# One decay in four moved from PSUM to SBUF for a fourth common PSUM bank, with the x projection ahead of the gates, a two-lane feed-forward and the second expert product by halves

## The chip, the cores and the metric

The kernel runs on one core of a Trainium2 chip, in fp32, as one launch. The metric is the device time in microseconds. Engines are named as the profile names them: PE (TensorE), PEld (its weight loads), DVE (VectorE), ACT (ScalarE), POOL (GpSimd) and SP (SyncE, which mainly issues DMAs).

## What is computed

Two "metaformer" layers on x of 4 batches, 384 channels, 32 x 32 positions. Each layer adds a token mixer and then a feed-forward part to x:

```python
x = x + _L0_conv_ref(_ln_c(x), ...)          # selective scan in four directions
t = _to_tokens(x)
t = t + _L0_ffn_ref(_ln_t(t), ...)           # 384 -> 1536 -> 384, weights are Kronecker products
x = _from_tokens(t, x)
x = x + _L1_conv_ref(_ln_c(x), ...)          # in_proj, causal conv, SiLU, selective scan, gate, out_proj
t = _to_tokens(x)
t = t + _L1_ffn_ref(_ln_t(t), ...)           # 4 experts, the best 2 for each token
```

The heart of both mixers is the selective scan over 1024 positions, with 16 states to a channel:

```python
dA = jnp.exp(dtt[..., None] * A)                         # decay
h = h * dA + (dtt * ut)[..., None] * bt[:, :, None, :]   # scan
y = jnp.einsum('bkdn,bkn->bkd', h, ct)                   # times C, summed over the 16 states
```

Layer 0 scans each batch in four directions (384 channels each). Layer 1 scans 768 channels once. The experts of layer 1 compute `gelu(x @ w1[e] + b1[e]) @ w2[e]` with w1 of 384 x 1536 and w2 of 1536 x 384.

## The kernel before, in words

**The scan as a stream of steps.** The scan is cut into 48 passes (a batch's half of 512 positions in one direction in layer 0, or a half of the channels in layer 1) and each pass into 12 steps: three groups of 128 channels by four groups of four states. That makes 576 steps. A step works on four tiles of 128 x 512, where a tile's partitions are 32 channels by 4 states. For each tile x of 0 to 3:

- ACT computes the decay, exp(dt * A), into `das[x]` (`decay`, L1497). The four `das` are PSUM banks.
- POOL has multiplied dt*u by B for the whole step before, in one instruction of 128 x 2048 into `s` in SBUF (`times_b`, L1491). Four such `s` go round in a ring.
- DVE runs the scan over the decay and `s` (`scan`, L1506). [...]
- DVE multiplies by C from PSUM into `s` (`times_c`, L1555), or POOL does it within `s` (`times_c_pool`, L1571). As a rule POOL takes the last tile alone (354 of 546 instructions), or the last two; in 30 steps DVE takes all four.
- PE sums the states of the four tiles into the bank `acc` (`add`, L1527). After four steps DVE gathers `acc` into the result.

Between passes' steps, ACT also keeps the last column as the state of the next half (`keep_state`, L1521).

**Everything else runs beside it.** Before a pass come the x projection (`prep_quad0`, `prep_quad1`: L579, L811) and the dt projection with softplus (`prep_pass`, L482 to L505); its results go to DRAM and are read back spread over partitions. In front of layer 1's scan of a batch stand the rest of layer 0 for that batch (`post0`: layer norm, GELU, adding x, layer norm, feed-forward in four rounds `ffn`, L649 to L706) and `prep1`: layer norm, then the in-projection and convolution of six chunks of 128 channels in two lanes `conv`, then the gates (z's half of the in-projection, SiLU, stored to DRAM) in two lanes `gate` (L766 to L789), and only then is the job `("pre", 1, b, h)` ended, for which layer 1's x projection waits. Behind the scan come `post1` (gate, out-projection, layer norm), `front` (routing of tokens to experts by indirect DMA), `experts` (blocks of 256 tokens, "pairs", or of 128, "lone" ones: 8 pairs and 3 lone blocks a batch) and `combine` (each token's two expert results, weighted).

**The order is made at build time.** A planner (`Plan`) runs an event simulation with hand-given costs (the numbers behind `yield PE, ...`), and emits each engine's instructions in the order it finds. The scan's steps are its main streams; the rest are lanes with ranks, experts lowest.[...]

**PSUM and other rooms.** There are eight banks: `acc`, four `das`, and three common ones in the free list `ps`, which all lanes use. An expert's bank is only taken if another stays free (`bank`, L1142), and the second product of a pair takes two at once (`bank(2)`, L1231), so all three must be free. When the scan is over, the `tail` job (L1463) gives the `das` to `ps`, and the scan's SBUF tiles to the lists of temporaries `tmp`, `t1` and of expert weights `mws`.

**Names of lines.** L1221 and L1241 are the experts' first and second products, L1187 their transposes, L1300 the copy of a block's result out of PSUM, L1332 and L1350 the indirect loads and products of `combine`. L671 and L682 are the feed-forward's products, L716 and L756 in-projection and convolution, L764 the convolution's SiLU, L780 and L783 the gates' copy and SiLU. L413 to L437 are layer norms, L1015 is a small cast in `front`. L1546 are products of zero weights that keep PE busy while it would wait (`fill`).

Of the kernel before, what the change touches and what calls it, by code (L numbers as in the profile page):

```python
# [36 lines left out]
NPAIR, NLONE = 8, 3  # L37
NBLK = NPAIR + NLONE
# [214 lines left out]
def layers(ctx, tc, ins, out, const):  # L253
# [47 lines left out]
    NK = T // P  # L301
    gates = {(b, h): wp.tile([P, NK, NE], F32, name=f"g{b}{h}") for b in range(NB) for h in range(NT)}
# [3 lines left out]
    tables = [wp.tile([1, 2, NBLK], I32, name=f"table{b}") for b in range(NB)]  # L306
    sels = tiles(2, [P, NK + 1, NE], "sel", pool=wp)
    b1s = tiles(3, [P, NF], "b1s", pool=wp)
    b2 = wp.tile([NE, D], F32, name="b2")
    nc.sync.dma_start(out=b2, in_=ins["b2"])  # L310
# [19 lines left out]
    pair_of = numbers(*range(NPAIR), 99, NPAIR, NPAIR)  # L330
    pair_at = numbers(*(2 * P * i for i in range(NPAIR)), 0, 2 * P * NPAIR, 2 * P * NPAIR + P)
    lone_of = numbers(*(NLONE + i for i in range(NPAIR)), *range(NLONE))
    floats = numbers(*[1] * NPAIR, *[0] * NLONE)
# [4 lines left out]
    ones = wp.tile([P, P], F32, name="ones")  # L338
    nc.vector.memset(ones, 1.0)
# [6 lines left out]
    nil = wp.tile([P, QP], F32, name="nil")  # L346
    nc.vector.memset(nil, 0.0)
    das = tiles(NG, [P, T], "da", pool=ps_1)
    ps = Free(tiles(3, [P, T], "ps", pool=ps_1))
# [42 lines left out]
    slot_y = [dram.tile([NE * SLOTS, D], F32, name=f"ys{b}") for b in range(NB)]  # L392
# [8 lines left out]
    def piece(dram_ap, c, h):  # L401
        return dram_ap[c * P : (c + 1) * P, cols(h)]
# [206 lines left out]
    def post0(b, h):  # L609
# [10 lines left out]
        def gelu():  # L620
            yield ACT, 3 * 0.82 + SWITCH
            for c in range(NC):
                nc.scalar.activation(y[:, c], y[:, c], AF.Gelu, bias=pv("lnb0", c, 1), scale=pv("lnw0", c, 1))
            exp_set()

        def add_x():
            for c in range(NC):
                xh = yield from t1.take()
                yield SP, land(256)
                nc.sync.dma_start(out=xh, in_=piece(x_in[b], c, h))  # L630
                yield POOL, 1.3
                nc.gpsimd.tensor_tensor(y[:, c], y[:, c], xh, ALU.add)
                t1.give(xh)

# [20 lines left out]
        def ffn():  # L655
            zg = st["zg", b]
            for i in range(NF // NC):
                w, proj1 = yield from wts.two()
                yield SP, land(192)
                nc.sync.dma_start(  # L660
                    out=w.rearrange("p a m -> p (a m)")[zrow, :], in_=ins["w_fc1"][:, i * NC * P : (i + 1) * NC * P]
                )
                nc.sync.dma_start(
                    out=proj1[:, :, :32],
                    in_=ins["w_proj1"][i * NC * P : (i + 1) * NC * P].rearrange("(f p) i -> p f i", p=P),
                )
                hid = yield from tmp.take()
                for j in range(NC):
                    ph = yield from ps.take()
                    yield PE, 1.1  # L670
                    nc.tensor.matmul(ph, lhsT=w[zrow, j, :], rhs=zg[zrow], start=True, stop=True)  # L671
                    yield ACT, 0.6
                    nc.scalar.copy(hid[:, j, :], ph)
                    ps.give(ph)
                wts.give(w)
                yield ACT, 1.5 + SWITCH
                nc.scalar.activation(hid, hid, AF.Gelu)
                exp_set()
                pr = yield from ps.take()
                yield PE, 3.0  # L680
                for j in range(NC):
                    nc.tensor.matmul(pr[grow], lhsT=proj1[:, j, :32], rhs=hid[:, j, :], start=j == 0, stop=j == NC - 1)  # L682
                tmp.give(hid)
                wts.give(proj1)
                if i == 0:
                    yield ACT, 0.6
                    nc.scalar.copy(zg[grow], pr[grow])
                else:
                    yield DVE, 0.65
                    nc.vector.tensor_tensor(zg[grow], zg[grow], pr[grow], ALU.add)  # L690
                ps.give(pr)
# [16 lines left out]
        return [ln1, gelu, add_x, ln2, ffn]  # L708
# [9 lines left out]
    def prep1(b, h):  # L718
# [6 lines left out]
        def conv(i):  # L725
            def gen():
                for j in range(NC):
                    c = i * NC + j
                    w, dg = yield from wts.two()
                    yield SP, land(192)  # L730
                    nc.sync.dma_start(out=w, in_=w_in[:, :, c * P : (c + 1) * P])
# [3 lines left out]
                    dg4 = yield from t1.take()  # L735
                    taps = [dg[:, 0, :], dg[:, 1, :], dg[:, 2, :], dg4[:, :P]]
# [21 lines left out]
                    wts.give(dg)  # L758
                    t1.give(dg4)
# [36 lines left out]
        return [ln, [conv(0), conv(1)], [gate(0), gate(1)], end]  # L796
# [114 lines left out]
    def front(u):  # L911
# [3 lines left out]
        def gen():  # L915
            b, h = u
# [82 lines left out]
            for j in range(NK):  # L999
                nc.tensor.matmul(  # L1000
                    pc[:, (j + 1) * NE : (NK + 1) * NE].rearrange("p (j e) -> p j e", e=NE),
                    lhsT=ones,
                    rhs=rep(sel[:, j], NK - j),
                    start=False,
                    stop=j == NK - 1,
                )
            yield DVE, 1.2
            so_far = nexts[b % 2] if h else base
# [3 lines left out]
            nc.vector.tensor_tensor(nexts[b % 2], pc[:, NK * NE : (NK + 1) * NE], so_far, ALU.add)  # L1012
# [3 lines left out]
            if h == NT - 1:  # L1016
                yield DVE, 6.0
                blocks(b, scratch, pg)
# [3 lines left out]
            yield from till(lambda: ("zero",) in plan.end and (b < 2 or ("read", b - 2) in plan.end))  # L1022
            t = 0.0
            for j in range(NK):
# [10 lines left out]
                for k in range(2):  # L1035
                    t = 3.0 + (yield POOL, 1.05, max(t, sent))
                    nc.gpsimd.indirect_dma_start(
                        out=slot_x[b % 2],
# [9 lines left out]
    def blocks(b, scratch, pg):  # L1048
# [26 lines left out]
        def within(at, first, end):  # L1075

            out, below = room("s", 1, NBLK, NE), room("p", 1, NBLK, NE)
            tt(out, lay(at, NE, True), lay(first[:1], NBLK, False), ALU.is_ge)
            tt(below, lay(at, NE, True), lay(end[:1], NBLK, False), ALU.is_lt)
# [4 lines left out]
        tt(cnt, nexts[b % 2], base, ALU.subtract)  # L1084
# [18 lines left out]
        tt(of_pair, of_pair, lay(off[:1], NBLK, False), ALU.mult)  # L1103
        at_pair = total("p", of_pair)
        at_s, number = room("s", 1, NBLK), room("p", 1, NBLK)
# [3 lines left out]
        last, number_s, no_pair = room("s", 1, 1), room("s", 1, NBLK), room("s", 1, NBLK)  # L1109
# [4 lines left out]
        tt(of_lone, of_lone, lay(off_lone[:1], NBLK, False), ALU.mult)  # L1114
# [4 lines left out]
        tt(of_lone, lay(at_lone, NE, True), lay(base[:1], NBLK, False), ALU.is_ge)  # L1119
        expert = total("p", of_lone)  # L1120
        nc.vector.tensor_scalar(expert, expert, -1.0, None, ALU.add)
        nc.vector.tensor_copy(tables[b][:, 0], at_lone)
        nc.vector.tensor_copy(tables[b][:, 1], expert)

    def experts():
        every = [(b, i) for b in range(NB) for i in range(NBLK)]
        size = [2] * NPAIR + [1] * NLONE
# [6 lines left out]
        def pressing():  # L1134

            done = [("gather", p0[NB - 1, 0]) in plan.end, ("pre", 1, NB - 1, 1) in plan.end]
            return done == [True, False]

        def known(b):
            return till(lambda: ("route", (b, NT - 1)) in plan.end)  # L1140
# [6 lines left out]
        def weights():  # L1147

            for b, i in every:
                yield from known(b)  # L1150
                yield SP, 1.0
                e = nc.sync.value_load(tables[b][:, 1, i : i + 1], min_val=0, max_val=NE - 1)
# [7 lines left out]
        def fetch():  # L1160

            for n, (b, i) in enumerate(every):
                yield from known(b)
# [3 lines left out]
                m = size[i]  # L1167
# [3 lines left out]
                yield SP, land(393), max(plan.end["route", (b, h)] for h in range(NT))  # L1171
                at = nc.sync.value_load(tables[b][:, 0, i : i + 1], min_val=0, max_val=NE * SLOTS - m * P)
                nc.sync.dma_start(
                    out=row, in_=slot_x[b % 2][bass.DynSlice(at, m * P)].rearrange("(s p) d -> p s d", p=P)
                )
                e = nc.sync.value_load(tables[b][:, 1, i : i + 1], min_val=0, max_val=NE - 1)
# [3 lines left out]
                if i == NBLK - 1:  # L1180
                    plan.end["read", b] = plan.now
# [18 lines left out]
        def work():  # L1200

            for n, (b, i) in enumerate(every):
# [4 lines left out]
                m = size[i]  # L1207
# [4 lines left out]
                for q in range(NQ):  # L1212
# [4 lines left out]
                    t = yield PE, 0.25 + 1.35 * m  # L1217
# [13 lines left out]
                py = (yield from bank(2)) if m == 2 else [(yield from bank())]  # L1231
                for q in range(NQ):
                    half_, at_ = divmod(2 * q, per)
                    yield from till(lambda: wq and half_ in made)
                    t, w = wq.pop(0)
                    yield "at", max(t, made[half_])
                    t = yield PE, 0.25 + 1.35 * m
                    w = w.rearrange("p (f d) -> p f d", f=2)
                    for f in range(2):
                        for k in range(m):  # L1240
                            nc.tensor.matmul(  # L1241
                                py[k][:, :D],
# [571 lines left out]
```

## Time and profile before

| What | Value |
|---|---|
| median of 3 runs (lowest to highest) | 5395.71 us (5385.36 to 5401.94) |
| the profiled execution | 5395.74 us, span 5394.0 us |
| mean granted TensorE clock | 0.918 |
| busy: PE, DVE, POOL, ACT | 4694.9, 4139.3, 3963.3, 3239.3 us |
| first and last scan instruction of the 48 passes | 82 (first `times_b`), 4567 us |
| `times_b` on POOL, L1491 | 576 x 4532 ns |
| scans on DVE, L1506, in PSUM | 801 x 1219 ns, 765 x 1286 ns (with a state) |
| scans on DVE, L1506, into SBUF | 351 x 1206 ns, 387 x 1275 ns (with a state) |
| products with C on DVE, L1555 | 1566 x 683 ns |
| decays on ACT, L1497 | 2304 x 686 ns |

How to read it: the first 4567 us are the stream of scan steps with everything else beside it; the last 827 us are the remaining experts and the combination of their results. Times in the text are in us from the span's start. A group's row has, after the bar, its busy time in us and the mean of one in ns. In the rows of stretches each engine's busy us stand with the number of its instructions, then the granted clock, the DMA share and GB/s. Records of neighbouring instructions of one engine overlap a little, so that their sum can exceed the time that they took.

### The profile page before, as it was taken

What the parts mean: (1) busy time and instruction counts of PE and PEld (TensorE: products, weight loads), DVE (VectorE), ACT (ScalarE), POOL (GpSimd) and SP (SyncE); (2) the same over time, 40 slices, a digit from 0 to 9 for tenths busy, and PEclk for the clock granted to TensorE, in tenths of its full rate; (3) what the DMA queues carried; (4) which work ended last, traced back from release to release, by engine and by line L of the source; (5) the groups of instructions that cost most, each with busy time, mean ns of one, the idle gap of its engine ahead of it and who ended that gap; (6) DMA issues with size and microseconds to landing.
All of it is one profiled execution on the core that took longest, in us unless ns stands there. A gap on an engine that the chain in (4) does not pass through costs nothing. (4 is left out here: it accounts for less than half of the span.)

```text
span 5394.0 us, 56734 instructions
## 1 busy us (share of the span) xinstructions
PE 4694.9 (87%) x17760; PEld 2159.8 (40%) x17760; DVE 4139.3 (77%) x4939; ACT 3239.3 (60%) x5776; POOL 3963.3 (73%) x1818
## 2 busy tenths in 40 slices
PE   9787787888888888989888888988899888999999
PEld 3222222222323333433444322333333345677776
DVE  5999999999999999488999999999993978100000
ACT  4454566765555777575666677776865645444342
POOL 4999998989898999388989889999983967200101
PEclk9889898899898989999999879999899999999998
DMA  3345555344444544546566444565534446556554
GB/s 123 126 153 187 186 190 188 123 157 145 151 137 150 185 150 138 164 154 200 180 197 215 148 130 147 170 201 172 166 126 148 153 171 204 174 179 216 168 172 160
DMA packets 425928, 890.56 MB, mean 165 GB/s; under 512 B 74485, under 2 KB 176025, under 8 KB 407193
## 3 DMA queue, kind: packets, MB, share of 16 engines
q1 hardware_dynamic: 368408, 695.53, 40.1%
q10 hardware_dynamic: 49024, 166.22, 8.9%
q0 software_dynamic: 8192, 25.17, 1.4%
q8 instruction: 141, 2.31, 0.2%
q14 instruction: 163, 1.33, 0.1%
HBM read 711.82 MB, written 174.95 MB: 164 GB/s over the span
## 5 line engine op out<-in xcount | busy, mean ns | idle before, releaser
L1491 POOL TENSOR_TENSOR s<-dtus,bt 128x2048 f32<-128x2048 f32 x576 | 2604.8, 4532 | 209.4 <-PE acc L1527 86.2
L1497 ACT ACTIVATE da<-dts,a 128x512 f32<-128x512 f32 x2304 | 1533.0, 686 | 1011.5 <-DVE s L1555 874.9
L1527 PE MATMUL acc<-s,four 128*32 128x512 f32 x4608 | 1062.9, 651 | 255.0 <-POOL s L1571 179.9
L1555 DVE TENSOR_TENSOR s<-da,ct 128x512 f32<-128x512 f32 x1566 | 1018.1, 683 | 51.3 <-ACT state L1521 50.6
L1546 PE MATMUL acc<-ident,nil 128*32 128x256 f32 x3980 | 978.5, 399 | 57.1 <-DVE big L601 22.3
L1571 POOL TENSOR_TENSOR s<-s,ct 128x512 f32<-128x512 f32 (+1 forms) x546 | 901.5, 1652 | 145.8 <-DVE s L1506 117.0
L1506 DVE TENSOR_TENSOR_SCAN da<-da,state,s 128x512 f32<-128x512 f32 x765 | 957.8, 1286 | 42.9 <-ACT ps L497 26.4
L1506 DVE TENSOR_TENSOR_SCAN da<-da,s 128x512 f32<-128x512 f32 x801 | 951.5, 1219 | 41.7 <-POOL s L1491 34.9
L1546 PEld LDWEIGHTS acc<-ident,nil 128*32 128x32 f32 x3980 | 436.7, 115 | 599.1 <-issue 183.0
L1527 PEld LDWEIGHTS acc<-s,four 128*32 128x32 f32 x4608 | 182.8, 111 | 834.2 <-POOL s L1571 395.8
L1506 DVE TENSOR_TENSOR_SCAN s<-da,state,s 128x512 f32<-128x512 f32 x387 | 484.3, 1275 | 0.1
L1506 DVE TENSOR_TENSOR_SCAN s<-da,s 128x512 f32<-128x512 f32 x351 | 417.3, 1206 | 4.9 <-ACT da L1497 4.8
L1221 PE MATMUL ps<-tmp,mw 128*128 128x256 f32 (+1 forms) x1728 | 376.6, 372 | 6.4 <-DVE tmp L413 2.2
L1241 PE MATMUL ps<-mw,tmp 128*128 128x384 f32 x1000 | 359.8, 505 | 8.6 <-DMA mw<-in_w_dram 4.9
L1221 PEld LDWEIGHTS ps<-tmp,mw 128*128 128x128 f32 x1728 | 305.9, 199 | 117.0 <-issue 28.7
L1355 DVE TENSOR_TENSOR tmp<-tmp,ps 128x384 f32<-128x384 f32 x16 | 8.8, 552 | 409.0 <-DMA dtus<-ys,slot 315.0
L1332 POOL DMA_INDIRECT tmp<-ys,slot x44 | 42.0, 956 | 370.0 <-ACT tmp L1342 319.9
L716 PE MATMUL ps<-big,w 128*128 128x512 f32 x576 | 285.8, 637 | 29.2 <-DMA w<-in_w_in_dram 17.6
L505 POOL TENSOR_TENSOR tmp<-tmp,big 128x256 f32<-128x256 f32 (+1 forms) x192 | 199.4, 1066 | 136.2 <-DVE tmp L499 136.1
L1241 PEld LDWEIGHTS ps<-mw,tmp 128*128 128x128 f32 x1000 | 187.9, 195 | 181.3 <-issue 54.0
L1355 DVE TENSOR_TENSOR s<-s,ps 128x384 f32<-128x384 f32 x2 | 1.1, 555 | 281.1 <-PE ps L1350 281.1
L482 PE MATMUL ps<-xd,dtw 12*128 12x512 f32 (+1 forms) x288 | 182.8, 718 | 30.1 <-DVE tmp L499 17.9
(364 smaller groups left out, 5703.0 us busy)
## 6 DMA issues: line engine op xcount, KB each, us to landing
mw<-in_w_dram SPq DMA_DIRECT2D x411, 384.0 KB
dtus<-dts SPq DMA_DIRECT2D x144, 1024.0 KB
dts<-dts ACTq DMA_DIRECT2D x288, 512.0 KB
dts<-tmp SPq DMA_DIRECT2D x384, 192.0 KB
bt<-rows SPq DMA_DIRECT2D x192, 256.0 KB
ct<-rows SPq DMA_DIRECT2D x192, 256.0 KB
dts<-in_w_dram SPq DMA_DIRECT2D x117, 384.0 KB
ys<-t SPq DMA_DIRECT2D x32, 768.0 KB
```

Of the source, the lines that this page charges most:

```text
L482: nc.tensor.matmul(pd, lhsT=dtw[dt_rows(q), c * P : (c + 1) * P], rhs=xd[dt_rows(q), cols(h)], start=True, stop=True,)
L505: nc.gpsimd.tensor_tensor(to, by, u[:, c], ALU.mult)
L716: nc.tensor.matmul(pi, lhsT=w[:, c, :], rhs=u[:, c], start=c == 0, stop=c == NC - 1)
L1221: nc.tensor.matmul(ph[:, k * width : (k + 1) * width], lhsT=w[:, c, k * P : (k + 1) * P], rhs=turned[:, c], start=c == 0, stop=c == NC - 1,)
L1241: nc.tensor.matmul(py[k][:, :D], lhsT=by_f(hids[half_], width)[:, at_ + f, k * P : (k + 1) * P], rhs=w[:, f], start=2 * q + f == 0, stop=2 ...
L1491: nc.gpsimd.tensor_tensor(ss[i % NSR], dtus[part_of(i) % 2], rep(bts[i % 4], NG), ALU.mult)
L1497: nc.scalar.activation(das[x], dts[(2 * part_of(i) + x // 2) % 3][:, x % 2, :], AF.Exp, scale=v["a"][:, g, m : m + 1])
L1506: nc.vector.tensor_tensor_scan(d if in_psum else s, d, s, 0.0 if v["first"] else state[:, v["slot"], j, x : x + 1], ALU.mult, ALU.add)
L1527: nc.tensor.matmul(acc[x * QP : (x + 1) * QP, :], lhsT=four, rhs=ss[i % NSR][:, x, :], start=m == 0, stop=m == 3)
L1546: nc.tensor.matmul(acc[:QP, : 2 * P], lhsT=nil, rhs=rep(ident, 2), start=fresh, stop=fresh)
L1555: nc.vector.tensor_tensor(ss[i % NSR][:, x, :], das[x], cts[i % 4], ALU.mult)
L1571: nc.gpsimd.tensor_tensor(s[:, m:, :], s[:, m:, :], rep(cts[i % 4], NG - m), ALU.mult)
```

## The change

1. `das[3]` becomes an SBUF tile, and `ps` has four banks. For the room in SBUF, some constants shrink to one column and are broadcast, `b2` is loaded at each combination, and the convolution's four tap matrices lie in one tile of `t1`, so a convolution takes one tile of `wts` in place of two.
2. `prep1` marks `("conv", b, h)` after the convolution's lanes; layer 1's x projection waits for this mark, and the gates come after it.
3. The feed-forward of `post0` runs as two lanes of two rounds each, in place of four rounds in a row; x is added by three lanes, which load it while the GELU is awaited.
4. The experts' second product is made in two halves of 192 columns. A half holds one bank, in which the two blocks of a pair lie side by side. The host lays w2 out accordingly.
5. Blocks are counted by groups of units (here a group is a batch, as before), the results' store has three buffers in place of four, and two planner costs and the copies' cost are set anew.

```diff
-    das = tiles(NG, [P, T], "da", pool=ps_1)
-    ps = Free(tiles(3, [P, T], "ps", pool=ps_1))
+    das = [*tiles(NG - 1, [P, T], "da", pool=ps_1), sp.tile([P, T], F32, name="da3")]
+    ps = Free(tiles(4, [P, T], "ps", pool=ps_1))
...
-    slot_y = [dram.tile([NE * SLOTS, D], F32, name=f"ys{b}") for b in range(NB)]
+    slot_y = [dram.tile([NE * SLOTS, D], F32, name=f"ys{g}") for g in range(3)]
...
-        def add_x():
-            for c in range(NC):
+        def add_x(c):
+            def gen():
                 xh = yield from t1.take()
                 yield SP, land(256)
                 nc.sync.dma_start(out=xh, in_=piece(x_in[b], c, h))
+                yield from till(lambda: ("gelu", b, h) in plan.end)
+                yield "at", plan.end["gelu", b, h]
                 yield POOL, 1.3
                 nc.gpsimd.tensor_tensor(y[:, c], y[:, c], xh, ALU.add)
                 t1.give(xh)
+
+            return gen
...
-        def ffn():
+        def ffn(lane):
+            def gen():
+                zg = st["zg", b]
+                for i in range(2 * lane, 2 * lane + 2):
...
-            for i in range(NF // NC):
...
-        return [ln1, gelu, add_x, ln2, ffn]
+        return [ln1, [gelu, *(add_x(c) for c in range(NC))], ln2, [ffn(0), ffn(1)], ffn_out]
...
-                    w, dg = yield from wts.two()
-                    yield SP, land(192)
-                    nc.sync.dma_start(out=w, in_=w_in[:, :, c * P : (c + 1) * P])
+                    w = yield from wload(w_in[:, :, c * P : (c + 1) * P])
...
-                    dg4 = yield from t1.take()
-                    taps = [dg[:, 0, :], dg[:, 1, :], dg[:, 2, :], dg4[:, :P]]
+                    dg = yield from t1.take()
+                    taps = [dg[:, tap * P : (tap + 1) * P] for tap in range(4)]
...
-        return [ln, [conv(0), conv(1)], [gate(0), gate(1)], end]
+        def mark():
+            plan.end["conv", b, h] = plan.now
+            return
+            yield
+
+        return [ln, [conv(0), conv(1)], mark, [gate(0), gate(1)], end]
...
-                py = (yield from bank(2)) if m == 2 else [(yield from bank())]
-                for q in range(NQ):
...
-                    t = yield PE, 0.25 + 1.35 * m
-                    w = w.rearrange("p (f d) -> p f d", f=2)
-                    for f in range(2):
-                        for k in range(m):
-                            nc.tensor.matmul(
-                                py[k][:, :D],
...
+                for part in range(2):
+                    py = yield from bank()
+                    for q in range(NQ // 2):
...
+                        t = yield PE, 0.1 + 1.32 * m
+                        w = w.rearrange("p (f d) -> p f d", f=4)
+                        for f in range(4):
+                            half_, at_ = divmod(4 * q + f, per)
+                            for k in range(m):
+                                nc.tensor.matmul(
+                                    py[:, k * HD : (k + 1) * HD],
...
+                    kq.append((t, g, i, part, py, at))
...
-                    yield ACT, 0.5
-                    nc.scalar.copy(row[:, :D], py[k][:, :D])
+                    yield ACT, 0.36 * m
+                    for k in range(m):
+                        nc.scalar.copy(rows[k][:, part * HD : (part + 1) * HD], py[:, k * HD : (k + 1) * HD])
...
+                b2 = flat[:NE, 2 * D + 3 * P :]
+                yield SP, land(6)
+                nc.sync.dma_start(out=b2, in_=ins["b2"])
...
-        q["need"] = ("pre", 0, b) if layer == 0 else ("pre", 1, b, x)
-        deps = [q["need"] if layer == 0 else ("pre", 1, b, x - 1) if x else ("post", 0, b, 0)] + ([("quad", n - 1)] if n else []) + ([("pass", p - 3)] if n > 1 else [])
+        q["need"] = ("pre", 0, b) if layer == 0 else ("conv", b, x)
+        deps = [q["need"] if layer == 0 else ("conv", b, x - 1) if x else ("post", 0, b, 0)] + ([("quad", n - 1)] if n else []) + ([("pass", p - 3)] if n > 1 else [])
...
-        ps.give(*das)
+        ps.give(*das[: NG - 1])
...
-        t1.give(*bts, *cts)
+        t1.give(*bts, *cts, das[NG - 1])
```

## The prediction, on record before the result

> **What bounds the kernel now.** I read the page's busy rows first, then the stretches between scan stops, then one plain step on VectorE and GpSimd.
>
> The page, busy tenths in 40 slices of 135 us: VectorE and GpSimd are full together until slice 34, then TensorE alone is.
>
> ```profile
> PE   9787787888888888989888888988899888999999
> DVE  5999999999999999488999999999993978100000
> POOL 4999998989898999388989889999983967200101
> ```
>
> The stretches (us, then busy us of PE, PEld, DVE, ACT, POOL): the two long stops of the scan, and what follows its last instruction at 4567.
>
> ```profile
> 2173.00:2256.00 83.00, 79.79 (x245) 38.51 (x243) 9.70 (x12) 42.36 (x70) 8.14 (x4) 0.98 0.59 188
> ...
> 4048.00:4159.00 111.00, 104.71 (x283) 44.09 (x281) 17.78 (x20) 51.56 (x77) 19.56 (x14) 0.98 0.53 167
> ...
> 4567.00:5394.00 827.00, 799.00 (x3418) 577.89 (x3416) 35.64 (x101) 331.97 (x566) 71.60 (x71) 0.95 0.58 181
> ```
>
> So the span is 82 us of start, 4485 us of scan (82 to 4567) and an 827 us tail that TensorE fills to 97%. In the scan lie five stops of 83, 33, 111, 33 and 12 us = 272 us; the other 4213 us carry 576 steps, 7.31 us each. In the same stretches without the four longer stops GpSimd is busy 1913.5 + 146.3 + 1455.7 + 155.6 + 166.7 = 3838 us, 6.66 us a step. Neither engine has much to give. A plain step, VectorE, then GpSimd:
>
> ```profile
> 3573.63 1.22 DVE L1506 TENSOR_TENSOR_SCAN da<-da,s 128x512 f32<-128x512 f32 x1
> 3574.76 1.20 DVE L1506 TENSOR_TENSOR_SCAN s<-da,s 128x512 f32<-128x512 f32 x1
> ...
> 3579.89 1.22 DVE L1506 TENSOR_TENSOR_SCAN da<-da,s 128x512 f32<-128x512 f32 x1
> ```
>
> ```profile
> 3572.88 4.53 POOL L1491 TENSOR_TENSOR s<-dtus,bt 128x2048 f32<-128x2048 f32 x1
> 3577.36 0.18 POOL L1570 COPY state<-s 128x1 f32<-128x1 f32 x1
> 3577.61 1.26 POOL L1571 TENSOR_TENSOR s<-s,ct 128x512 f32<-128x512 f32 x1
> ```
>
> The step is 6.26 us on VectorE (3573.63 to 3579.89) and 5.97 on GpSimd. The fourth scan (3574.76, `s<-da,s`) runs wholly inside GpSimd's `times_b` (3572.88 to 3577.41); GpSimd's `times_c` needs it next.
>
> **The fourth decay in SBUF.** This scan now reads both its streams, `da3` and `s`, from SBUF; until now every large VectorE operation had one operand in PSUM. The page has no such operation beside GpSimd. The nearest row is a small cast between two SBUF tiles, on VectorE and what GpSimd did then:
>
> ```profile
> 1645.19 3.30 DVE L1015 CAST slot<-t 128x8 int32<-128x8 f32 x1
> ```
>
> ```profile
> 1643.96 4.50 POOL L1491 TENSOR_TENSOR s<-dtus,bt 128x2048 f32<-128x2048 f32 x1
> ```
>
> Alone the cast takes 0.17 us. Here it ended at 1648.49, 0.03 after GpSimd's instruction (1648.46); at 2803 (1.83 us) and 4414 (2.04 us) it also ended 0.03 after the GpSimd instruction that was running. It was shut out for the whole instruction. That is one input in a copy, not two in a scan. [...] The scan rows of before, all with one input in PSUM, show no such wait (1.21 and 1.28 us). [...]
>
> Price: in the plain step GpSimd does 4.53 (`times_b`), then the fourth scan 1.15, hand-over about 0.25 (0.22 idle before the copy at 442.22, ended by the scan), then 0.18 + 1.26: 7.4 us in place of 6.26. Over all steps GpSimd's 6.66 + 1.15 + 0.25 = 8.06 us against 7.31: +0.75 x 576 = +430 us, the floor. On top come steps in which VectorE is the longer one all the same: around the waiting scan it has some 1.1 us of slack (7.4 - 6.26), and about 90 layernorm operations of 1.75 us exceed it by 0.65, +60; and GpSimd's own waits that are not this scan (136 us for L499's `tmp`, 86 for `acc`, 64 for `dtus`), of which I take some 110 to stay. Sum +600. The upper end: GpSimd's queue has 149 places where two `times_b` follow each other. If VectorE gets in only after both, it idles 3.4 us more at each of some 120: +400, so +1000. Behind the waiting scan stand on VectorE `mult` 2, the next step's scans and all gathers and layernorms; ACT's decays, `times_c`, TensorE's `add` and, through `acc` and the ring of four `s`, the next `times_b` wait for these. The 30 or so steps whose four products VectorE does itself (576 less 546 `times_c`) add a two-SBUF product of 0.68: within the rounding.
>
> Smaller: the decay's 0.69 us exponential writes SBUF, and the scan reads it there. [...] The trace has only the write side: 1206 ns to SBUF, 1219 to PSUM, -7 us. [...] ACT is 60% busy; a slightly longer exponential is hidden.
>
> **X projection ahead of the gates.** In the 83 us stop the last convolution's SiLU ends at 2160.9, the gates' six products and SiLUs run until 2190.5, the x projection (L811) starts at 2194.9. In the 111 us stop the same points are 4054.1, 4091.1, 4092.1. The gates' instructions (36 matmuls, 6 copies, SiLU, six weight loads on SP, a store on ACT's queue) all stay; they go beside the dt projection and the first scans, where TensorE waits for `add` and fills with idle products (L1546); on SP their weight loads now stand behind the pass's spreads, which costs nothing while post1 needs the gates only four passes (350 us) later. Without that cover the 33 to 37 us come back as a later end of the same chain. -33 and -37 us, and about as much in the two 33 us stops.
>
> **Two-lane feed-forward, add_x by three lanes, convolution with one weight tile in place of two.** Same instructions. In front of the 111 us stop one half's feed-forward runs from 3751 to 3893, 142 us for four rounds in a row; two lanes halve at most the waiting, -50 to -70, -40 where both halves compete for the four weight tiles. Together with the gates this exceeds each stop; the 50 us from x projection to first `times_b` (4098 to 4154) is next late and partly left. Of 272 us I take off 225 (bounds 120 and 265). The order is fixed at build time, so slower scans don't shorten the stops by themselves.
>
> **The fourth bank, second product by halves.** A pair of experts' blocks needed all three common banks free for its second product; now one of four suffices. Before, 33 of 76 result copies (L1300) were made by 4367, of 38 of the first two batches; those five are 2.5 pair blocks of 31 us (72 x 0.216 + 48 x 0.322 us, the chain's x24 5.18 and x16 5.16). That is 78 us that may leave the tail; I take -55. Against it: twice as many instructions of 192 columns for 384. By the chain's 0.216 us for 256 columns and 0.112 for 128 (x48 5.36) one takes 0.164: 96 x 0.164 = 15.7 for 15.5 us, +5 us in the tail. Weight loads double, but the 128-column case hides them already. So -50 (-130 to +60).
>
> At nothing: b2's 32 loads of 6 KB (issued before the indirect loads that take 3 us, so hidden; some 0.5 us of SP each if not), one store buffer fewer to zero, batch 3's results waiting for batch 0's combine (done by 3010), half-width copies (ACT is 40% busy in the tail).
>
> **Sum.** 5395.7 (span 5394.0 and 1.7 around it; the median is 5395.7 too) + 600 - 225 - 50 = 5720 us. About 0.3% (16 us) is what a measurement can tell from no change.
>
> **Rivals.**
> 1. VectorE slips in at each end of a GpSimd instruction, +600: 5720 (5600 to 5850). 0.47.
> 2. GpSimd's queued pairs go first: +880 to +1000: 5396 + 900 - 275 = 6020. For it: GpSimd's next instruction starts up to 0.04 us before the former's end. Against: the cast got in within 0.03. 0.19.
> 3. The floor, +430, and the whole 330 of gains: 5500. 0.15.
> 4. Not slower: the scan with two SBUF inputs does not wait for `times_b` (for it: no large row of before shows a two-input wait). Then 5396 - 225 - 50 - 20 = 5100. It decides from the point where the wait falls below 275 / 576 = 0.48 us a step. 0.17.
> The remaining 0.02 is a wait just at that point, no change.
>
> Faster 0.17, same 0.02, slower 0.81. The range leaves out case 4 and reaches from below case 3 into case 2: 5450 to 6080; the likeliest alone 5600 to 5850.
>
> **What would show it.** L1506 `s<-da` for the fourth decay with a mean of 2 us or more, where 1.21 and 1.28 stand now, each end 0.03 us behind an L1491; 7.4 us or more between L1491s in plain steps; the scan's end near 4940 and a tail near 780; stops of the scan under 50 us in sum; x projection within a few us of the convolution's SiLU. I am wrong if the fourth scan stays at 1.2 us (case 4), or if the steps pass 9 us (case 2). If the stops stay, the chain ahead of the convolution was late and not the gates.

## The result, and the profile after

The changed kernel takes 5878.35 us (median of 4 runs, 5874.78 to 5886.63) against 5390.53 us before (4 runs): the ratio is 1.0905 with a 95% interval of 1.088 to 1.093. It is slower by 9%. The profiled execution has a span of 5876.3 us.

The page of the changed kernel, busy tenths in 40 slices (of 147 us now). GpSimd, full before, is mostly at 7 to 8 in the scan; VectorE is at 9 nearly throughout, and of its dips at the long stops one is left.

```profile
PE   8777677787877788897878888888878877899999
...
DVE  5999999999999999996998999999999999610000
...
POOL 4878887888887887886787888888878788500101
```

Cut at the same places (first and last scan instruction; a stop is more than 3 us without a scan between two passes), the two spans differ like this. All values are read from the scans' times in the two traces:

| | first scan | stops | steps, us each | tail | span |
|---|---|---|---|---|---|
| before | 89 | 272 | 4207, 7.30 | 827 | 5394.0 |
| after | 90 | 57 | 4939, 8.57 | 790 | 5876.3 |
| difference | +1 | -215 | +732 | -36 | +482 |

TensorE's granted clock is lower too, 0.884 in the mean where it was 0.918. The steps don't wait for it: VectorE, which gathers TensorE's sums, is idle for 157 us of all the steps, 168 before.

VectorE's groups of the changed kernel (count, busy us, mean ns, idle before). The scans that write SBUF (their product with C is GpSimd's), 1206 and 1275 ns in the kernel before, are the ones to look at.

```profile
L1601 DVE TENSOR_TENSOR s<-da,ct 128x512 f32<-128x512 f32 x1560 | 1078.2, 719 | 30.6 <-ACT state L1567 30.1
L1552 DVE TENSOR_TENSOR_SCAN da<-da,s 128x512 f32<-128x512 f32 x799 | 972.7, 1245 | 11.7 <-ACT da L1543 7.9
L1552 DVE TENSOR_TENSOR_SCAN da<-da,state,s 128x512 f32<-128x512 f32 x761 | 956.9, 1286 | 25.1 <-POOL s L1537 14.6
L1552 DVE TENSOR_TENSOR_SCAN s<-da,state,s 128x512 f32<-128x512 f32 x391 | 791.0, 2043 | 5.3 <-ACT da L1543 5.3
L1552 DVE TENSOR_TENSOR_SCAN s<-da,s 128x512 f32<-128x512 f32 x353 | 722.2, 2062 | 0.4 <-ACT da L1543 0.4
```

These two rows hold third tiles as well, whose decay is still in PSUM. Of the fourth tile alone (every fourth scan in order) the mean is 2.36 us, 1.24 before, and 384 of the 576 exceed 1.45 us. A waiting instruction counts as busy here: the waits stand in its duration, not in the idle column (5.3 and 0.4 us for the last two rows). That is why VectorE looks full.

One such scan, on VectorE and then what GpSimd did:

```profile
4416.93 1.22 DVE L1552 TENSOR_TENSOR_SCAN da<-da,s 128x512 f32<-128x512 f32 x1
4418.06 3.11 DVE L1552 TENSOR_TENSOR_SCAN s<-da,s 128x512 f32<-128x512 f32 x1
```

```profile
4415.57 4.51 POOL L1537 TENSOR_TENSOR s<-dtus,bt 128x2048 f32<-128x2048 f32 x1
4421.23 0.18 POOL L1616 COPY state<-s 128x1 f32<-128x1 f32 x1 [1.15 <-DVE s L1552]
```

`times_b` ends at 4420.08, the scan at 4421.17, 1.09 us later: it did its work only then. GpSimd meanwhile stood idle for 1.15 us, as its next instruction needs this scan. It also goes the other way. Here the scan has waited for the end of `times_c` at 4060.40 and goes first, and the `times_b` that comes second takes 5.43 us in place of 4.53:

```profile
4060.01 1.46 DVE L1552 TENSOR_TENSOR_SCAN s<-da,s 128x512 f32<-128x512 f32 x1
```

```profile
4058.05 2.35 POOL L1617 TENSOR_TENSOR s<-s,ct 128x1024 f32<-128x1024 f32 x1
4060.35 5.43 POOL L1537 TENSOR_TENSOR s<-dtus,bt 128x2048 f32<-128x2048 f32 x1
```

All 384 long scans end 1.08 us after the end of a GpSimd instruction, within 0.014 us; only 7 let another boundary between two GpSimd instructions pass first. 323 of them began inside `times_b`. What the fourth scans take beyond 1.25 us sums to 640 us of waiting.

### The profile page after: what moved, and what is told of

It is laid out like the page before. It is cut to its first block, busy times and chain, and to the rows that moved or that the text cites. A ratio compares the mean times of both kernels' runs of the same rounds, so it can differ in the third digit from the quotient of the medians.

```text
span 5876.3 us, 60149 instructions
## 1 busy us (share of the span) xinstructions
PE 4864.8 (83%) x19390; PEld 2455.7 (42%) x19390; DVE 4864.0 (83%) x4933; ACT 3252.2 (55%) x5850; POOL 4120.6 (70%) x1811
## 5 line engine op out<-in xcount | busy, mean ns | idle before, releaser
L1537 POOL TENSOR_TENSOR s<-dtus,bt 128x2048 f32<-128x2048 f32 x576 | 2682.1, 4665 | 178.3 <-PE acc L1573 127.6
L1573 PE MATMUL acc<-s,four 128*32 128x512 f32 x4608 | 1161.5, 674 | 445.6 <-POOL s L1617 206.3
L1601 DVE TENSOR_TENSOR s<-da,ct 128x512 f32<-128x512 f32 x1560 | 1078.2, 719 | 30.6 <-ACT state L1567 30.1
L1552 DVE TENSOR_TENSOR_SCAN s<-da,state,s 128x512 f32<-128x512 f32 x391 | 791.0, 2043 | 5.3 <-ACT da L1543 5.3
L1552 DVE TENSOR_TENSOR_SCAN s<-da,s 128x512 f32<-128x512 f32 x353 | 722.2, 2062 | 0.4 <-ACT da L1543 0.4
L1253 PE MATMUL ps<-tmp,mw 128*128 128x256 f32 (+1 forms) x1872 | 402.8, 372 | 22.0 <-DVE tmp L511 9.0
L1275 PE MATMUL ps<-mw,tmp 128*128 128x192 f32 x2144 | 392.8, 340 | 11.5 <-ACT tmp L1321 10.1
L1275 PEld LDWEIGHTS ps<-mw,tmp 128*128 128x128 f32 x2144 | 364.9, 198 | 73.7 <-issue 39.3
L1401 DVE TENSOR_TENSOR tmp<-tmp,ps 128x384 f32<-128x384 f32 x19 | 10.4, 547 | 352.5 <-PE ps L1396 348.3
L1616 POOL COPY state<-s 128x1 f32<-128x1 f32 (+1 forms) x269 | 51.6, 192 | 321.5 <-DVE s L1552 316.8
L780 PE MATMUL ps<-tmp,t 128*128 128x512 f32 x384 | 200.4, 671 | 44.2 <-ACT tmp L773 40.8
```

What stands on the lines that cost most here:

```text
L780: nc.tensor.matmul(pk, lhsT=taps[tap], rhs=xt[:, tap : tap + T], start=tap == 0, stop=tap == 3)
L1253: nc.tensor.matmul(ph[:, k * width : (k + 1) * width], lhsT=w[:, c, k * P : (k + 1) * P], rhs=turned[:, c], start=c == 0, stop=c == NC - 1,)
L1275: nc.tensor.matmul(py[:, k * HD : (k + 1) * HD], lhsT=by_f(hids[half_], width)[:, at_, k * P : (k + 1) * P], rhs=w[:, f], start=4 * q + f ...
L1537: nc.gpsimd.tensor_tensor(ss[i % NSR], dtus[part_of(i) % 2], rep(bts[i % 4], NG), ALU.mult)
L1552: nc.vector.tensor_tensor_scan(d if in_psum else s, d, s, 0.0 if v["first"] else state[:, v["slot"], j, x : x + 1], ALU.mult, ALU.add)
L1573: nc.tensor.matmul(acc[x * QP : (x + 1) * QP, :], lhsT=four, rhs=ss[i % NSR][:, x, :], start=m == 0, stop=m == 3)
```

## The experiments

Each run's time is a median; the span of its profiled execution is cut as above. The base for all ratios is the kernel before on the same chip.

| Run | Time, us | stops | us a step | tail |
|---|---|---|---|---|
| decays in PSUM, three banks | 5299.22 | 85 | 7.41 | 847 |
| fourth decay in SBUF alone | 6074.48 | 288 | 8.49 | 809 |
| after, three banks | 5958.17 | 82 | 8.56 | 849 |
| after, `times_b` in two | 5730.89 | 47 | 8.34 | 787 |
| after, `times_b` only writes | 5211.48 | 31 | 7.47 | 786 |
| x projection ahead alone | 5352.60 | 214 | 7.35 | 832 |
| lanes alone | 5325.67 | 158 | 7.38 | 821 |
| both, product whole | 5355.84 | 101 | 7.38 | 908 |
| lanes and halves | 5312.17 | 130 | 7.41 | 830 |
| three decays in turn, four banks | 5332.07 | 63 | 7.62 | 795 |
| the same, ACT's side work patient | 5485.48 | 257 | 7.54 | 794 |

### All decays back in PSUM, three common banks

```diff
-    das = [*tiles(NG - 1, [P, T], "da", pool=ps_1), sp.tile([P, T], F32, name="da3")]
-    ps = Free(tiles(4, [P, T], "ps", pool=ps_1))
+    das = tiles(NG, [P, T], "da", pool=ps_1)
+    ps = Free(tiles(3, [P, T], "ps", pool=ps_1))
```

> The changed kernel with all four decays back in PSUM and three common banks; the rest of the change stays. Theory A (the two-SBUF scan is shut out while GpSimd's instruction runs): the 696 us of waits of VectorE go, steps are back near 7.3 us, the stops stay short, 5100 to 5220 us. Rival B (the steps are longer because the fourth bank lets more side work and experts between them): without the fourth bank the stops come back to 150 us or more and the steps shorten too, 5250 to 5400 us. Rival C (the chain edits themselves are worth nothing): 5380 to 5400.

5299.22 us, ratio 0.984 (0.983 to 0.986). Steps fall from 8.57 to 7.41 us, (8.57 - 7.41) x 576 = 670 us, and the stops stay short at 85 us. VectorE's groups of this run:

```profile
L1552 DVE TENSOR_TENSOR_SCAN s<-da,state,s 128x512 f32<-128x512 f32 x390 | 486.3, 1271 | 3.6 <-ACT da L1543 3.5
L1552 DVE TENSOR_TENSOR_SCAN s<-da,s 128x512 f32<-128x512 f32 x364 | 432.7, 1207 | 5.0 <-ACT da L1543 4.9
```

So the loss goes with the SBUF decay, and the rest of the change gains 1.6% even without the fourth bank. The time is 80 us above theory A's range: stops 85 and a tail of 847, both longer than with the fourth bank. The expectation had counted neither.

### The fourth decay in SBUF alone

The same move in the kernel before, with three common banks and one bank unused. The small constants and `b2` are as in the change: without them the scan's tiles would need 202.03 KB of SBUF a partition, and 200.22 are left.

```diff
-    das = tiles(NG, [P, T], "da", pool=ps_1)
+    das = [*tiles(NG - 1, [P, T], "da", pool=ps_1), sp.tile([P, T], F32, name="da3")]
```

> The kernel before with only the fourth decay in SBUF (and, for its room there, the small constants as single columns and b2 loaded at each combination); three common banks, the freed one unused, the instruction order that of before. Theory A (the two-SBUF scan is shut out while GpSimd's instruction runs): steps of 8.45 to 8.6 us, stops near 270 and tail near 827 as before, 6040 to 6130 us, and the fourth scan at a mean of 2.2 us or more. Rival B (the longer steps come of the fourth bank and the side work it lets in): under +150, 5400 to 5540 us.

6074.48 us, ratio 1.127 (1.125 to 1.130), as theory A has it. Rival B, that side work through the fourth bank lengthens the steps, is out: the side work is that of before here, and the steps are 8.49 us, 683 us more in all. The fourth scan's mean is 2.39 us. The two rows that hold it, third tiles included:

```profile
L1507 DVE TENSOR_TENSOR_SCAN s<-da,state,s 128x512 f32<-128x512 f32 x387 | 780.1, 2037 | 0.1
L1507 DVE TENSOR_TENSOR_SCAN s<-da,s 128x512 f32<-128x512 f32 x344 | 731.3, 2141 | 0.8 <-ACT da L1498 0.8
```

### The changed kernel with three common banks

```diff
-    ps = Free(tiles(4, [P, T], "ps", pool=ps_1))
+    ps = Free(tiles(3, [P, T], "ps", pool=ps_1))
```

> The changed kernel with three common banks in place of four, the fourth decay still in SBUF, one bank unused. If the bank is worth what the run with all decays in PSUM lacked (stops 85 for 57 us, tail 847 for 790), the time is 5878 + 85 = 5940 to 5990 us with steps near 8.6 us. Rival B (the bank's side work lengthens the steps): steps fall under 8.3 us and the time to 5800 or less. If the bank does nothing: 5870 to 5890.

5958.17 us (ratio 1.106). Steps are unchanged (8.56), stops +25, tail +58: the bank is worth 80 us. That is what it was bought for; its price was 670.

### times_b in two instructions

```diff
-        nc.gpsimd.tensor_tensor(ss[i % NSR], dtus[part_of(i) % 2], rep(bts[i % 4], NG), ALU.mult)
+        for g in range(0, NG, 2):
+            of = slice(g, g + 2)
+            nc.gpsimd.tensor_tensor(ss[i % NSR][:, of], dtus[part_of(i) % 2][:, of], rep(bts[i % 4], 2), ALU.mult)
```

> The changed kernel with times_b as two instructions of 128x1024 in place of one of 128x2048. Theory A: the longest wait behind it halves from 4.5 to 2.3 us and VectorE gets in between the two; the waits fall from 640 us to 350 to 450, against some 50 us more on GpSimd for the second instruction: 5650 to 5800 us. [...]

5730.89 us, ratio 1.064 (1.062 to 1.066), 147 us under the changed kernel. The waits fall from 640 to 491 us, less far than expected. Behind `times_b` a wait is 1.22 us in the mean where it was 1.83, but there are as many of them (343, 323 before). Part of the gain goes back on GpSimd: its waits for the scan fall from 674 to 354 us, but 262 of its 1152 halves take over 2.5 us where 2.36 is the rule, 231 us in all (77 us with whole `times_b`). The length of the instruction matters, and each of the 431 long scans still ends 1.08 us behind the end of a GpSimd instruction.

### times_b that only writes

```diff
-        nc.gpsimd.tensor_tensor(ss[i % NSR], dtus[part_of(i) % 2], rep(bts[i % 4], NG), ALU.mult)
+        for _ in range(2):
+            nc.gpsimd.memset(ss[i % NSR], 0.5)
```

> The changed kernel with times_b replaced by two memsets of the same tile on GpSimd: the product of dt*u and B is left out, so that GpSimd only writes SBUF in that place; times_c still reads. If a GpSimd instruction that reads is what shuts the two-SBUF scan out: no wait of the fourth scan behind the memsets, those behind times_c and the dt*u products stay (0.3 us or less a step in the mean, fourth scan under 1.6 us). If any GpSimd instruction does: waits behind the memsets too, each as long as what is left of the memset, fourth scan near 2 us.

5211.48 us in one run; the product of dt*u and B is left out. The fourth scan's mean is 1.28 us and its waits sum to 28 us (640 in the changed kernel). GpSimd is less full, 3474 us busy for 4121, but its memsets still run beside the scans: 219 fourth scans began with more than 0.3 us of a memset still to run, and took 1.23 us in the mean and 1.29 at most. All 35 that exceed 1.45 us waited behind a GpSimd instruction that reads SBUF. ACT still writes the fourth decay to SBUF here, so that write is not the cause. The memsets, and then the fourth scans with the third tiles on VectorE:

```profile
L1538 POOL MEMSET s<- 128x2048 f32 x1152 | 2073.4, 1805 | 266.0 <-PE acc L1574 220.5 <-DVE da L1553 10.5 <-PE acc L1593 1.3
```

```profile
L1553 DVE TENSOR_TENSOR_SCAN s<-da,state,s 128x512 f32<-128x512 f32 x391 | 499.3, 1298 | 7.7 <-ACT da L1544 7.7
L1553 DVE TENSOR_TENSOR_SCAN s<-da,s 128x512 f32<-128x512 f32 x353 | 429.4, 1234 | 2.6 <-ACT da L1544 2.0 <-ACT state L1568 0.4
```

So in this run the scan was held up by GpSimd instructions that read SBUF (all 35 waits that bring a scan over 1.45 us), not by the memsets, which only write it (1.29 us at most). The small cast, on which the prediction leaned, behaves otherwise: one of these waited behind a memset, on VectorE and then on GpSimd:

```profile
2789.31 0.56 DVE L1043 CAST slot<-t 128x8 int32<-128x8 f32 x1
```

```profile
2786.17 3.67 POOL L1538 MEMSET s<- 128x2048 f32 x2
```

It ends 0.03 us behind the memset, at 2789.87. So the cast's wait is not that of the scan, and the cast was no proof of it.

The run also gives the size of the fourth rival: the change without its waits is 5211 us here, not 5100. The run with all decays in PSUM says the same: 5299 less the 80 us of the bank is 5219.

### X projection ahead alone, lanes alone, and both

The kernel before with only the mark behind the convolution:

```diff
-        return [ln, [conv(0), conv(1)], [gate(0), gate(1)], end]
+        return [ln, [conv(0), conv(1)], mark, [gate(0), gate(1)], end]
```

> The kernel before with only the x projection ahead of the gates. By the prediction's working: 30 to 37 us off each of the four longer stops, 260 us of stops to some 130: 5250 to 5290 us. Rival (the convolution's end is late for the feed-forward ahead of it, and the gates' products move into the next chain): under 50 us gained, 5345 or more.

5352.60 us, ratio 0.993 (0.992 to 0.995): 33 us, a quarter of what was expected, as the expectation's rival has it. The x projection does move: in the first long stop it ends at 2147.6, 2.8 us behind the convolution's SiLU. But `times_b` starts at 2230 only. TensorE after it, in this run (L816 is the x projection, L716 the gates' products, L482 the first dt projection):

```profile
2144.86 2.78 PE L816 MATMUL ps<-big,w 128*56 128x512 f32 x6 [0.33 <-ACT big L764]
...
2149.45 5.42 PE L716 MATMUL ps<-big,w 128*128 128x512 f32 x12
...
2161.25 7.08 PE L716 MATMUL ps<-big,w 128*128 128x512 f32 x12 [2.60 <-DMA w<-in_w_in_dram]
...
2172.05 1.12 PE L482 MATMUL ps<-xd,dtw 24*128 24x512 f32 x2
```

Two thirds of the gates go ahead of the dt projection. From the x projection's end to `times_b` it now takes 82 us, where it took 51 before (2200.3 to 2251.7), as the lines of the kernel before and then `times_b` of both show. Of these 31 us, 14 lie ahead of the first dt projection (24.4 us for 10.4); the other 17 lie behind it and were not taken apart.

```profile
2194.89 5.36 PE L811 MATMUL ps<-big,w 128*56 128x512 f32 x12
...
2210.69 1.12 PE L482 MATMUL ps<-xd,dtw 24*128 24x512 f32 x2
```

```profile
2251.66 8.98 POOL L1491 TENSOR_TENSOR s<-dtus,bt 128x2048 f32<-128x2048 f32 x2 [18.79 <-DMA dtus<-dts]
```

```profile
2229.94 8.98 POOL L1496 TENSOR_TENSOR s<-dtus,bt 128x2048 f32<-128x2048 f32 x2 [21.00 <-DMA dtus<-dts]
```

The stop of 83 us became 78, that of 111 became 82, those of 33 became 17 and 37.

The lanes (feed-forward, adding x, one weight tile in the convolution) without the mark and without halves:

> The kernel before with only the two-lane feed-forward, the three lanes that add x and the convolution with one weight tile; decays in PSUM, three common banks, second product whole, gates ahead of the x projection. With the run of the x projection alone (stops 272 to 214 us) and the run of both (stops 101, tail 908) it makes a square. If the two add up: stops near 160 us, and the time 5355 to 5385 us as the tail grows by most of what the stops lose. If each stop is set by the later of two chains, so that only both together shorten it: stops over 200 us, 5375 or more.

5325.67 us, ratio 0.989 (0.986 to 0.992). The two stops of 83 and 111 us are down to 10 and 8; what is left, 46 and 81 us, stands before the second halves' passes. The time is 30 us below the expected range, as the tail did not grow (821). Stops add up (-58 and -114, together -171), times don't: both together, with the product whole, gave 5355.84 us (ratio 0.994), because the tail grew to 908 us.

> The run with all decays in PSUM and three common banks, with the second expert product as before (whole, two banks for a pair). If halves help with three banks (one bank of two free, in place of three of three): fewer copies done before the scan's end, a tail over 880 us, 5330 to 5400 us. If they only cost their instructions in the tail: 5280 to 5295 us. Stops and steps within 20 us of the run with halves either way.

The halves bring that tail to 847 and the time down by 57 us: beside the scan 31 of 76 results were made without them, 36 with them (72 half copies). This fits the bank that a half doesn't hold, though without the mark they make one result more only (38 for 37). Their instructions cost nothing that shows: 16 of 192 columns take 2.60 us, 0.1625 each.

Lanes and halves without the mark:

> The run with all decays in PSUM and three common banks (5299 us), with the gates again ahead of the x projection: lanes and halves alone. The x projection ahead took 33 us by itself, but on top of the lanes it shortened the stops by 57 us and lengthened the tail by 87. If halves mend that tail (907.9 to 847.0 us with x ahead), x ahead is worth its 57 us of stops less some tail: this version 5310 to 5350 us. If the experts' time beside the scan is what counts: 5270 to 5295 us, with a tail under 810.

5312.17 us, ratio 0.984 (0.982 to 0.986): within noise of the version with the mark, and half a per cent below the lanes alone. On top of lanes and halves the x projection ahead takes 45 us off the stops and gives 17 back in the tail, and no gain can be told.

### Three decay banks in turn, with four common banks

A way to keep the bank and all decays in PSUM: the n-th tile of the whole stream takes bank n mod 3, and a decay waits for the tile three before it.

```diff
+    def bank_of(i, x):
+        return das[(NG * i + x) % 3]
...
-            free = [("da free", i - 1, x)] if i else []
+            k, y = divmod(NG * i + x - 3, NG)
+            free = [("da free", k, y)] if k >= 0 else []
```

> The changed kernel with three decay banks in PSUM used in turn (tile n of all tiles takes bank n mod 3), no decay in SBUF, and the four common banks kept. Theory A: no wait behind GpSimd; with the bank's 85 us it would give 5299 - 85 = 5215 us if decays come in time. The rival for this version: a decay can start only when the tile three before it is through, so that ACT has some 0.6 to 1 us in hand where it had 2.4 or more, and each longer instruction of ACT (GELU, table loads, some 130) holds VectorE up by 2 us: 5400 to 5500 us, with L1506's successor idle on ACT's decays.

5332.07 us, ratio 0.989 (0.987 to 0.991), between the two cases expected. The bank pays (stops 63, tail 795), but steps are 7.62 us, +0.21 x 576 = 119 us against the run with four decay banks. VectorE's waits in this run say why:

```profile
DVE da L1555 <- ACT da L1546: 123.5, 52, 8.5
DVE s L1555 <- ACT da L1546: 97.4, 43, 9.5
```

Letting ACT's side work wait 14 us in place of 6 brings these to 78.3 and 72.8 us, but the chains ahead of layer 1 get late and the stops are back at 257 us: 5485.48 us, ratio 1.017, 85 us above the worse case expected.

> The run with three decay banks in turn and four common banks (5332 us), with the planner letting side work on ACT wait 14 us in place of 6 before it goes ahead of the decays. If ACT's side work is what holds the decays up (123.5 + 97.4 us of VectorE's idle time): those fall under 120 us and the steps to 7.5 us, 5260 to 5310 us, unless the chains ahead of layer 1 get late (stops over 120 us), then 5330 to 5400.

The fastest versions found are the change with its decays left in PSUM and three common banks, with or without the x projection ahead: ratio 0.984.

## Why the prediction was right, and where its terms were off

The direction, the mechanism and the range held: 5878 in 5450 to 6080, though above the likeliest case's own 5600 to 5850.

- **The fourth scan waits for `times_b`: right, but priced on the wrong engine.** That it would wait was the author's estimate from the cast; the longest fourth scan before took 1.35 us. +600 was forecast for the steps, +732 came. The move made 670 of these (8.57 against 7.41 us a step with all decays in PSUM); the other 62 came with the new side work, which the forecast put at nothing. The forecast followed GpSimd's step, 8.06 us for 7.31, and gave VectorE 1.1 us of slack around the waiting scan. VectorE has no such slack. In the two longest stretches of steps, before and then after, it is busy 96 to 97% (the length, then PE, PEld, DVE):

```profile
82.00:2173.00 2091.00, 1725.26 (x6477) 644.41 (x6476) 2006.45 (x2293) 1292.46 (x2330) 1913.49 (x846) 0.90 0.47 157
2449.00:4048.00 1599.00, 1380.15 (x5051) 576.79 (x5050) 1529.79 (x1753) 1107.69 (x1971) 1455.68 (x640) 0.90 0.52 170
```

```profile
90.00:2696.00 2606.00, 2052.66 (x7420) 800.44 (x7417) 2538.99 (x2469) 1452.70 (x2637) 2151.36 (x924) 0.87 0.43 138
2740.00:5086.00 2346.00, 1920.92 (x7354) 921.88 (x7354) 2254.38 (x2232) 1422.95 (x2565) 1881.40 (x806) 0.88 0.48 156
```

Over all steps VectorE's busy time grows by 742 us, 640 of them the scan's waits, and its idle time falls by 11 only: the steps got longer by the whole of the waits. A third of the scans did not wait (when 176 of these 192 began, no GpSimd instruction had more than 0.3 us left to run), and two thirds waited 1.67 us in the mean. GpSimd is not full: its waits for this scan grew from 169 (117 and 52) to 674 us, as its two rows in the list of waits show. That the sum came near is in part luck.

```profile
POOL s L1617 <- DVE s L1552: 357.1, 201, 10.3
...
POOL state L1616 <- DVE s L1552: 316.8, 196, 7.0
```

- **Queued pairs of `times_b` (rival 2): its premise is wrong.** 45 of the long scans waited in a `times_b` with another right behind it. In all 45 the scan went in between, and in 42 the second `times_b` then took over 5 us. The time came near that rival by the sum of the waits, not by its mechanism.
- **The products of two SBUF tiles "within the rounding": not quite.** L1601 rose from 683 to 719 ns in the mean, 56 us over 1560 instructions. 26 of them, all fourth products with two SBUF inputs (32 in all), exceed 0.9 us, up to 9.9; the others take 670 ns.
- **The 1.15 us of the fourth scan in the price, and the -20 us in rival 4's sum: no run shows them.** Fourth scans of `s<-da,s` that did not wait (under 1.3 us) take 1203 ns in the mean in the changed kernel and in the run whose `times_b` only writes, as with the decay in PSUM before (1203), so reading the decay from SBUF saved nothing; one that waited ends 1.08 us behind the GpSimd instruction. On ACT the fourth tile's decay rose from 678 to 713 ns, hidden as forecast.
- **Stops -225: right in sum (-215), wrong in its parts, so the sum is in part luck.** The step that failed is that the gates "go beside the dt projection and the first scans, where TensorE waits for `add`". The planner put most of them ahead of it, and most of the gain was lost again within the stop: -58 alone, where some -140 was forecast. The lanes gave -114 alone.
- **Bank and halves -50: right in sum (-36).** The bank alone takes 58 us off the tail. The halves' instructions cost what was worked out (0.164 us, 0.1625 measured).
- **Rival 4's price was 110 us too low.** Even with no waits the steps are 7.41 to 7.47 us with the new side work, not under 7.3.
- **The signs.** The fourth scan's mean (2.36 us), the tail (790) and six of eight x projections within 7 us of the convolution's SiLU came as named. The scan's end is 5086 in place of 4940, and the stops are 57 us, not under 50. The long scans' ends lie 1.08 us behind a GpSimd instruction, not 0.03: that was read from the cast, which is short, while the scan still has its own work to do after the wait.

Why 384 scans wait, and for 1.67 us, is described by the traces, not derived: both engines' orders were planned for a machine without the wait, and no run tried a planner that knows it.

## What to carry to other kernels

Before an operand is moved from PSUM to SBUF, look at which engine reads it and what its other operand is: here a VectorE scan that got two SBUF inputs was put in line with GpSimd instructions that read SBUF (384 of 576 waited, 1.67 us in the mean). Both engines paid, with 640 us of waits on VectorE and 505 us more on GpSimd; price such a wait on the engine that has no idle time. A freed bank was worth 80 us here and its price 670. A step that is moved out of the way of a chain is only out of the way if the order behind it, here a planner's, really lets the chain go first: read the instruction that follows.

## What the hardware showed that was not expected

- In the profile the wait lies inside the waiting instruction's duration, on both engines: the fourth scan takes 2.36 us in the mean in place of 1.24, `times_b` up to 5.6 us in place of 4.5, with no idle time for it and no releaser. Only the ends, 1.08 us after a GpSimd instruction's end, tell it from slow work.
- The memsets on GpSimd, which only write SBUF, did not hold the scan up: beside 1152 of them, of 1.8 us, the waits are 28 us in all, and those over 0.2 us stand behind the GpSimd instructions that still read. A small cast did wait for a memset, 0.56 us where it takes 0.17 alone.
